# Two attention layers on one core: four score tiles in one run, and long products in 64-column halves

## The chip, the cores and the metric

The kernel runs on one core of one Trainium2 chip. The metric is the device time in microseconds of one execution. Three runs of the kernel before took 3401.60, 3404.48 and 3403.71 us; the median is 3403.71.

## What is computed

32 batches of 512 rows with 512 features go through two layers. All data and products are 32-bit floats.

```python
# layer 0, 8 heads of 64 columns
q, k, v = heads(x @ Wq.T + bq), heads(x @ Wk.T + bk), heads(x @ Wv.T + bv)
logits = q @ k.T / sqrt(64) + log(clip(adj, 1e-8))
out = softmax(logits) @ v                   # (512, 512) per batch
x = layer_norm(x + out @ Wo.T + bo, gamma, beta)
# layer 1, one head
p = x @ fc_w.T + fc_b
qq, kk = p @ q_w.T + q_b, p @ k_w.T + k_b
masked = leaky(qq + kk.T + (1 - adj) * -1e9)
x = softmax(masked) @ p + x
```

## The kernel before

**Slots.** The work of a batch b is divided into four slots, p = 0 to 3, one for each pair of heads (`slot`, L1258). The order of the instructions on each engine is the order in which the program writes them: nothing rearranges it. In one slot the attention of batch b, the end of layer 0 and layer 1 of batch b - 1, and the last products of batch b - 2 are mixed. A slot in the middle of the run takes about 26 us, a batch 105.

**Scores and values.** `score` (L825) multiplies 128 keys with 512 queries for two heads, one on the upper and one on the lower 64 rows of TensorE's array, and ScalarE makes the exponentials of both in one instruction (L836). There are four score tiles in a slot, kc = 0 to 3. `factors` (L839) multiplies them on VectorE by the adjacency, and `sums` (L849) adds them up. `values` (L859) multiplies with v; here the two heads lie on two column tiles of 64 columns each and are accumulated in one bank, `po`. Its second part ends with a copy on ScalarE (L877). The values used in a slot are those of the slot before.

**Divide.** `divide` (L880) sums over keys for four heads, on four column tiles of 32, copies the result (L892) and sends it through DRAM into another shape. `divided` (L900) inverts it and loads it as R, which has one buffer; `scale` (L920) multiplies it in.

**Long products.** Every other product of 512 x 512 matrices is done by a scheme with seven products of half size in place of eight. It needs sums and differences of quarters on VectorE before and after. Each product is written as four matmuls, each with a 128 x 128 left factor and 256 moving columns; the profile shows each as two instructions with two weight loads. They are the queries and keys of the next slot (`seven_qk`, L621, tiles `f`), the values of the next batch (`seven_v`, `pv`), the output projection (`seven_wo`, `pw`), the last product (`seven_out`, `pw_o`), all three through `seven` at L215, and the product with the layer 1 weights (`seven_z`, L998, `pw_z`). `differences` (L594, L602 to L605) makes the quarters of the next batch's x at the beginning of slot 3, for `seven_v` and `seven_qk`.

**Banks.** [...] The pool `ps_s` has two buffers of two banks, for the scores and the tiles `f`; `po` has one; the pool `ps_m` has three, which the other long products and the divide take in turn. A product's three results are called a, b and c. The output projection is seeded with a bias by two copies on ScalarE (`seed`, L749).

**Order of a slot.** TensorE gets: score tiles 0 and 1, the values of the slot before (both parts), score tiles 2 and 3, a divide in slots 0 and 2, then the long products. In slot 2, `layer1_rows` (L1391) orders the rest: sums of batch b for kc 0 and 1 (L1407), the sums for the last product (`z_sums`), dots for layer 1 (`ks`, `qs`), and the last product with its adds. The end of it is this line, and slot 3 begins with the differences:

```python
1439            run(muls[2:3] + adds[2] + muls[3:])
1440            load_e(last, 1)
1441            run(adds[3][:1] + qs + adds[3][1:])
```

DMAs are issued by SyncE, in the order of the program.

Of the kernel before, what the change touches and what calls it, by code (L numbers as in the profile page):

```python
# [9 lines left out]
FP = mybir.dt.float32  # L10
# [9 lines left out]
P = 128  # L20
# [10 lines left out]
def kernel(  # L31
# [173 lines left out]
    def turn_fc():  # L205

        fc12, fc22 = K["fc"][:, :KH, H:], K["fc"][:, KH:, H:]
        nc.vector.tensor_sub(fc12, fc22, fc12)

    def seven(data, weights, i, to, first, ns=range(KH)):  # L210


        for n in ns:
            for c in range(KH):
                nc.tensor.matmul(  # L215
                    to[:, n, :], data(i, c)[:, ts(n, P)], weights[i][:, c, :],
                    start=(first and n == 0 and c == 0),
                    stop=(n == KH - 1 and c == KH - 1), skip_group_check=True,
                )
# [278 lines left out]
    def fast(ctx):  # L498
# [4 lines left out]
        ps_o = ctx.enter_context(tc.tile_pool(name="ps_o", bufs=1, space=bass.MemoryType.PSUM))  # L503
        ps_m = ctx.enter_context(tc.tile_pool(name="ps_m", bufs=3, space=bass.MemoryType.PSUM))
        dram = ctx.enter_context(tc.tile_pool(name="dram", bufs=2, space=bass.MemoryType.DRAM))

        S = [dict() for _ in range(B)]

        def load_x(b):
# [98 lines left out]
        def seven_qk(b, p):  # L608

            qk_tiles(b, p)  # L610
            s = S[b]
            q, k = s["qT", p], s["kT", p]
            bq, bk = K["bq"][:, p : p + 1], K["bk"][:, p : p + 1]
            wq, wk, W = K["wq"], K["wk"], K["qk_s"]
            left = {1: wq[:, :KH], 2: wq[:, KH:], 3: W[:, 2], 4: wk[:, KH:],
                    5: W[:, 0], 6: W[:, 1], 7: wk[:, :KH]}
            ps = {}

            def mul(i, to, first):
                for c in range(KH):  # L620
                    nc.tensor.matmul(  # L621
                        to, left[i][:, c, ts(p, P)], s["B"][i][:, c, :],
                        start=(first and c == 0), stop=(c == KH - 1),
                        skip_group_check=True,
                    )

            def banks():
                f = [ps_s.tile([P, 2, N], FP, tag="s", name=f"f_{b}_{p}_{i}") for i in range(2)]
                for i, name in enumerate("acbd"):
                    ps[name] = f[i % 2][:, i // 2, :H]  # L630

            def unit0():
                banks()
                mul(1, ps["a"], True)
                mul(5, ps["c"], True)
                nc.scalar.copy(ps["b"], ps["a"])
                nc.scalar.activation(k[:, H:], ps["c"], AF.Identity, bias=bk)

            def unit1():
                mul(6, ps["a"], False)
                mul(2, ps["b"], False)
                nc.scalar.activation(q[:, H:], ps["a"], AF.Identity, bias=bq)  # L644
                nc.scalar.activation(q[:, :H], ps["b"], AF.Identity, bias=bq)

            def unit2():
                mul(4, ps["d"], True)
                mul(3, ps["c"], False)
                nc.scalar.activation(k[:, :H], ps["d"], AF.Identity, bias=bk, scale=-1.0)  # L650

            def adds():
                nc.vector.tensor_add(q[:, H:], ps["c"], q[:, H:])
                nc.vector.tensor_add(k[:, H:], ps["a"], k[:, H:])
                nc.vector.tensor_add(k[:, :H], ps["a"], k[:, :H])  # L655
            return [unit0, unit1, unit2, lambda: mul(7, ps["a"], False), adds]

        def seven_v(b):
# [13 lines left out]
            def unit0():  # L672
                for name in "abc":
                    ps[name] = ps_m.tile([P, KH, H], FP, tag="m", name=f"pv_{b}_{name}")
                mul(1, ps["a"], True)
# [59 lines left out]
        def seven_wo(b, banks, apart=False):  # L735
# [12 lines left out]

            def seed():  # L749
                for name, bank in zip("bac", banks()):  # L750
                    ps[name] = bank
                for name, h in (("a", 0), ("c", 1)):
                    bo = K["bo"][:, ts(h, H)].unsqueeze(1).to_broadcast([P, KH, H])
                    nc.scalar.copy(ps[name], bo)

# [11 lines left out]
        def seven_out(b):  # L767
# [30 lines left out]
            muls, adds = seven_rows(data, sub, K["fc_s"], K["fc"], lambda n: ps[n], add, True)  # L798
            muls[0] = lambda unit=muls[0]: unit0(unit)
            adds[2].insert(1, lambda: store(0))  # L800
            adds[3].append(lambda: store(1))
# [10 lines left out]
        def long_banks(b):  # L812
            return lambda: [
                ps_m.tile([P, KH, H], FP, tag="m", name=f"pw_{b}_{name}") for name in "bac"
            ]
# [8 lines left out]

        def score(b, p, kc):  # L825

            s = S[b]
            sc = ps_s.tile([P, 2, N], FP, tag="s", name=f"sc_{b}_{p}_{kc}")
            for j in range(2):
                rows = slice(j * DK, (j + 1) * DK)  # L830
                nc.tensor.matmul(  # L831
                    sc[:, j, :], s["kT", p][rows, ts(kc, P)], s["qT", p][rows, :],
                    start=True, stop=True,
                )
            at = act.tile([P, 2, N], FP, tag="at", name=f"at_{b}_{p}_{kc}", bufs=6)
            nc.scalar.activation(at, sc, AF.Exp, scale=SCALE)  # L836
            s["at", p, kc] = at
# [42 lines left out]
        def divide(b, p):  # L880


            s = S[b]
            ps = ps_m.tile([P, N], FP, tag="m", name=f"ps_{b}_{p}")
            for h in range(4):
# [93 lines left out]
        def seven_z(b):  # L979
# [15 lines left out]
            def mul(i, name, first=False):  # L995
                for m in range(KH):
                    for t in range(KH):
                        nc.tensor.matmul(  # L998
                            ps[name][:, m, :].rearrange("p (c n) -> p c n", c=KH),
                            left[i][:, t, ts(m, P)], right[i][:, :, ts(t, P)],  # L1000
                            start=(first and m == 0 and t == 0),
                            stop=(m == KH - 1 and t == KH - 1), skip_group_check=True,
                        )
# [58 lines left out]
        def find_range():  # L1062
# [19 lines left out]
            def over_partitions():  # L1082
                one = ps_s.tile([P, 2, N], FP, tag="s", name="one")
                nc.tensor.transpose(one[:1, 0, :2], least, ident[:2, :2])
                bad = const.tile([1, 1], FP, name="bad")
                nc.vector.tensor_reduce(bad, one[:1, 0, :2], AX.X, ALU.min)
                flag = const.tile([1, 1], I32, name="flag")
# [22 lines left out]
        def last_layer1(b):  # L1110
# [47 lines left out]
            def rest(range_steps, add_before):  # L1158
                ps = {}

                def mul(i, name, first=False):
                    for m in range(KH):
                        for t in range(KH):
                            nc.tensor.matmul(
                                ps[name][:, m, :], left[i][:, t, ts(m, P)], right[i][:, t, :],
                                start=(first and m == 0 and t == 0),
                                stop=(m == KH - 1 and t == KH - 1), skip_group_check=True,
                            )
# [89 lines left out]
        def slot(b, p):  # L1258
# [8 lines left out]
            if p == 3:  # L1267
                differences(nxt)
            for kc in (0, 1):
                score(b, p, kc)  # L1270
            if p == 1 and last >= 0:
                wos, wo_adds = seven_wo(last, long_banks(last))
                run(wos[:1])
            run(values(b, p - 1) if p > 0 else values(last, 3) if last >= 0 else first_v[1:2])
            if p == 0 and last >= 0:
                scale(last, 0)
                first_difference(last)
            factors(b, p, 0)
            fc_sums = right_units(K["fc"], K["fc_s"]) if b == 1 and p == 1 else []
            if p == 1:  # L1280
                sums(b, p, 0)
                run(fc_sums[:1])
                if last >= 0:
                    scale(last, 2)
                    first_sum(last)
            if p == 2 and last >= 0:
# [6 lines left out]
            for kc in (2, 3):  # L1293
                score(b, p, kc)
            soft = softmax(last) if p == 3 and last >= 0 else []
            run(soft[:1])
            if p == 0 and last >= 0:
                if b >= 2:
                    run(eT(b - 2))
                divide(last, 2)  # L1300
                if b == 1:
# [3 lines left out]
            if p == 3 and last >= 0:  # L1305
                divided(b, 0)
            if p == 2 and b != 1:
                divide(b, 0)
            if p < 3:
# [64 lines left out]
            if p == 3:  # L1374
# [11 lines left out]
                vs[3]()  # L1386
                turn_a((0, 1))
                sums(b, p, 0)
                sums(b, p, 1)

        def layer1_rows(b, next_qk, norm):  # L1391
# [11 lines left out]
            if b == 1:  # L1403
                run(next_qk[2:4])
                divide(b, 0)
            else:
                sums(b, 2, 0)  # L1407
# [31 lines left out]
            run(muls[2:3] + adds[2] + muls[3:])  # L1439
            load_e(last, 1)  # L1440
            run(adds[3][:1] + qs + adds[3][1:])

# [5 lines left out]
        def last_slot(rest):  # L1448
# [11 lines left out]
            for kc in (2, 3):  # L1460
                score(b, 3, kc)
            factors(b, 3, 1)
# [246 lines left out]
```

## Time and profile before

| | |
|---|---|
| median of three runs | 3403.71 us |
| span of the profiled execution | 3402.3 us |
| TensorE matmuls, busy | 3388.8 us, 15358 instructions |
| VectorE, busy | 3013.1 us |
| ScalarE, busy | 1393.7 us |
| score matmuls, L831 | 2048 instructions, 508.8 us |
| value matmuls, L869 | 2048 instructions, 468.1 us |
| divide matmuls, L886 | 504 instructions, 67.1 us |
| a long matmul's weight load of 128 columns, mean | 190 ns |
| a value matmul's weight load of 64 columns, mean | 136 ns |
| an exponential of 128 x 1024, L836, mean | 1022 ns |
| SyncE's queue, DMA share of 16 engines' span | 36.0% |

The busy time of a group is the time in which at least one of its instructions is under way; matmuls overlap, so the mean of one is longer than the step from one to the next. The chain of waits is counted from the end of one instruction to the end of the next. PE stands for TensorE's matmuls, PEld for its weight loads, DVE for VectorE, ACT for ScalarE, SP for SyncE.

### The profile page before, as it was taken

The page shows a single profiled execution, that of the slowest core. Times are in us where ns is not written, and L with a number is a line of the kernel's source. Part 1 is how long each engine was busy: PE and PEld are TensorE (multiplying, and loading weights), DVE is VectorE, ACT ScalarE, POOL GpSimd, SP SyncE. Part 2 cuts the span into 40 slices and gives each one's busy share as a digit, 9 for nine tenths or more (in the row PEclk, how much of TensorE's full clock was granted, in tenths as well). Part 3 has the DMA queues.
Part 4 walks back from the last instruction along what each step waited for, and adds up shares of the span by engine and source line. Part 5 has one row for each costly group of instructions (what it writes and reads, how often), then busy time and mean ns, then how long its engine had stood idle before and what let it go on. Part 6 is the DMA issues. An engine that isn't in the chain of part 4 may idle for free.

```text
span 3402.3 us, 43006 instructions
## 1 busy us (share of the span) xinstructions
PE 3388.8 (100%) x15358; PEld 2350.1 (69%) x15358; DVE 3013.1 (89%) x5284; ACT 1393.7 (41%) x2375; POOL 0.9 (0%) x9
## 2 busy tenths in 40 slices
PE   9999999999999999999999999999999999999999
PEld 5667667776777677766776677667766777677766
DVE  7888989889898898898898988989889898899888
ACT  3443443434433444434444343443444443444433
POOL 0000000000000000000000000000000000000000
PEclk9999999999999999999999999999999999999999
DMA  5234242343333443323424234343343333442321
GB/s 124 54 63 91 60 90 67 57 91 81 70 73 52 88 85 65 81 65 68 91 60 86 67 61 90 66 85 66 57 91 81 69 74 54 85 90 61 81 66 51
DMA packets 881572, 251.48 MB, mean 74 GB/s; under 512 B 806732, under 2 KB 809036, under 8 KB 881352
## 3 DMA queue, kind: packets, MB, share of 16 engines
q1 hardware_dynamic: 881352, 248.67, 36.0%
q8 instruction: 123, 2.02, 0.3%
q14 instruction: 97, 0.79, 0.1%
HBM read 182.46 MB, written 34.65 MB: 64 GB/s over the span
## 4 chain that ended last, share of the span: by engine, by line
PE 97%; DVE 1%; SPq 1%; ACT 0%; DMA 0%; issue 0%; DVEq 0%; ACTq 0%
PE f L621 22%; PE sc L831 14%; PE po L869 13%; PE pw_a L215 7%; PE pw_z_a L998 6%; PE pv_a L215 5%; PE pw_o_a L215 5%; PE pw_c L215 3%; PE pv_b L215 3%; PE pv_c L215 3%; PE pw_o_c L215 3%; PE pw_z_c L998 3%; PE pw_o_b L215 3%; PE ps L886 2%; PE pw_b L215 2%; PE pw_z_b L998 2%
## 5 line engine op out<-in xcount | busy, mean ns | idle before, releaser
L836 ACT ACTIVATE at<-sc 128x1024 f32<-128x1024 f32 x512 | 496.6, 1022 | 601.0 <-PE sc L831 599.8
L844 DVE SCALAR_TENSOR_TENSOR at<-cT,at 128x1024 f32<-128x1024 f32 x512 | 600.3, 1215 | 12.9 <-ACT at L836 12.5
L831 PE MATMUL sc<-qT,kT 64*128 64x512 f32 x2048 | 508.8, 615 | 0.5 <-DVE kT L655 0.4
L869 PE MATMUL po<-at,v 128*64 128x512 f32 x2048 | 468.1, 599 | 0.4 <-DVE at L844 0.3
L831 PEld LDWEIGHTS sc<-qT,kT 64*128 64x128 f32 x2048 | 178.0, 186 | 267.3 <-issue 267.3
L869 PEld LDWEIGHTS po<-at,v 128*64 128x64 f32 x2048 | 135.4, 136 | 317.4 <-issue 313.4
L857 DVE TENSOR_TENSOR as<-as,at 128x1024 f32<-128x1024 f32 x254 | 310.3, 1222 | 5.4
L621 PE MATMUL f<-xT,wq 128*128 128x256 f32 x1016 | 267.4, 386 | 0.5 <-ACT at L836 0.5
L621 PE MATMUL f<-T,qk_s 128*128 128x256 f32 x1016 | 250.3, 379 | 0.0
L621 PEld LDWEIGHTS f<-xT,wq 128*128 128x128 f32 x1016 | 187.7, 190 | 77.1 <-ACT at L836 54.2
L998 PE MATMUL pw_z_a<-eP,n 128*128 128x256 f32 x960 | 226.9, 379 | 1.0 <-DVE n L1035 1.0
L621 PEld LDWEIGHTS f<-T,qk_s 128*128 128x128 f32 x1016 | 192.5, 190 | 27.0 <-ACT at L836 0.4
L998 PEld LDWEIGHTS pw_z_a<-eP,n 128*128 128x128 f32 x960 | 180.2, 190 | 28.2 <-ACT L L1010 1.3
L877 ACT COPY oT<-po 128x512 f32<-128x512 f32 x128 | 75.2, 587 | 288.9 <-PE po L869 288.9
L854 DVE TENSOR_TENSOR as<-at,at 128x1024 f32<-128x1024 f32 x128 | 155.0, 1211 | 1.1
L644 ACT ACTIVATE qT<-f,bq 128x256 f32<-128x256 f32 x127 | 59.6, 469 | 223.5 <-PE f L621 223.5
L650 ACT ACTIVATE kT<-f,bk 128x256 f32<-128x256 f32 x127 | 59.8, 471 | 198.1 <-PE f L621 198.1
L762 DVE TENSOR_TENSOR n<-pw_a,n 128x512 f32<-128x512 f32 x96 | 66.3, 691 | 74.9 <-PE pw_a L215 74.9
L621 PE MATMUL f<-xT,qk_s 128*128 128x256 f32 x508 | 130.4, 379 | 0.0
L621 PE MATMUL f<-T,wk 128*128 128x256 f32 x508 | 130.4, 379 | 0.0
L621 PE MATMUL f<-xT,wk 128*128 128x256 f32 x508 | 130.4, 379 | 0.0
L215 PE MATMUL pv_a<-wv,xT 128*128 128x256 f32 x512 | 124.2, 385 | 0.0
(304 smaller groups left out, 5809.0 us busy)
## 6 DMA issues: line engine op xcount, KB each, us to landing
cT<-in_adj_dram SPq DMA_DIRECT2D x512, 64.0 KB
R<-d SPq DMA_DIRECT2D x126, 256.0 KB
x<-in_x_dram SPq DMA_DIRECT2D x124, 256.0 KB
n<-in_x_dram SPq DMA_DIRECT2D x31, 1024.0 KB
L<-in_adj_dram SPq DMA_DIRECT2D x60, 512.0 KB
eP<-L SPq DMA_DIRECT2D x480, 64.0 KB
out_dram<-yb SPq DMA_DIRECT2D x58, 512.0 KB
w<-dk SPq DMA_DIRECT2D x32, 256.0 KB
```

The lines of the kernel that those rows point to most:

```text
L215: nc.tensor.matmul(to[:, n, :], data(i, c)[:, ts(n, P)], weights[i][:, c, :], start=(first and n == 0 and c == 0), stop=(n == KH - 1 and c ...
L621: nc.tensor.matmul(to, left[i][:, c, ts(p, P)], s["B"][i][:, c, :], start=(first and c == 0), stop=(c == KH - 1), skip_group_check=True,)
L762: nc.vector.tensor_add(to, ps[name], to)
L831: nc.tensor.matmul(sc[:, j, :], s["kT", p][rows, ts(kc, P)], s["qT", p][rows, :], start=True, stop=True,)
L836: nc.scalar.activation(at, sc, AF.Exp, scale=SCALE)
L844: nc.vector.scalar_tensor_tensor(at, cT[:, kc, :].unsqueeze(1).to_broadcast([P, 2, N]), ADJ_MIN, at, ALU.max, ALU.mult,)
L854: nc.vector.tensor_add(s["as", p], s["at", p, 0], s["at", p, 1])
L857: nc.vector.tensor_add(s["as", p], s["as", p], s["at", p, kc])
L869: nc.tensor.matmul(s["po", p][j * DK : (j + 1) * DK, :], s["v"][h // 4][:, kc, ts(h % 4, DK)], s["at", p, kc][:, j, :], start=(kc == 0), s ...
L877: nc.scalar.copy(s["oT"][p], s["po", p])
L886: nc.tensor.matmul(ps[h * BL : (h + 1) * BL, :], ones[:, :BL], s["as", p + h // 2][:, h % 2, :], start=True, stop=True,)
L998: nc.tensor.matmul(ps[name][:, m, :].rearrange("p (c n) -> p c n", c=KH), left[i][:, t, ts(m, P)], right[i][:, :, ts(t, P)], start=(first ...
```

## The change

It has these parts.

1. A function `halves` writes a matmul with a 128-column left factor as two, each with 64 of the columns and with its own half of the output's partitions. All long products of the seven-product scheme use it.
2. The first part of the values goes ahead of score tiles 0 and 1 and the second part behind score tiles 2 and 3; all four score tiles follow each other on TensorE.
3. The third score tile (kc = 2) goes to two single banks, with two exponentials of 512 columns. The first slot and the last one keep the two-bank tile.
4. The pool `ps_m` becomes three fixed tiles, `lone`. The divide always uses `lone[0]`, the third score tile `lone[1]` and `lone[2]`, and the long products take a, c and b in this order; after the last product the list is turned by one.
5. In slot 1, the seed of a goes ahead of the values and that of c behind their second part, and `scale(last, 2)` and `first_sum` go ahead of the factors.
6. The divide goes between score tiles and the values' second part. In slot 0, that puts it ahead of the transposes of `eT` in the program.
7. In slot 3, `turn_a((0, 1))` goes behind the sums. In slot 2, the sums for kc 0 and 1 go from the beginning of `layer1_rows` to between the two halves of the last adds, where b > 1 and the batch is not the last.

```diff
+    def halves(to, left, right, start, stop):
+        for h in range(2):
+            nc.tensor.matmul(
+                to[ts(h, DK)], left[:, ts(h, DK)], right,
+                start=start, stop=stop, skip_group_check=True,
+            )
...
         for n in ns:
             for c in range(KH):
-                nc.tensor.matmul(
+                halves(
                     to[:, n, :], data(i, c)[:, ts(n, P)], weights[i][:, c, :],
-                    start=(first and n == 0 and c == 0),
-                    stop=(n == KH - 1 and c == KH - 1), skip_group_check=True,
+                    first and n == 0 and c == 0, n == KH - 1 and c == KH - 1,
                 )
...
+        ps_l = ctx.enter_context(tc.tile_pool(name="ps_l", bufs=1, space=bass.MemoryType.PSUM))
+        lone = [ps_l.tile([P, N], FP, name=f"m{i}") for i in "xyz"]
+        class Turns:
+            n = 0
+            def tile(self, shape, dtype, **_):
+                self.n += 1
+                return lone[self.n % 3]
+        ps_m = Turns()
...
+            muls[3] = lambda unit=muls[3]: (unit(), lone.insert(0, lone.pop()))
...
         def long_banks(b):
             return lambda: [
-                ps_m.tile([P, KH, H], FP, tag="m", name=f"pw_{b}_{name}") for name in "bac"
+                lone[i].rearrange("p (n f) -> p n f", n=KH) for i in (2, 0, 1)
             ]
...
+        def score(b, p, kc, apart=False):
+            s = S[b]
+            halved = kc == 2 and not apart
+            if halved:
+                parts = lone[1:]
+            else:
+                sc = ps_s.tile([P, 2, N], FP, tag="s", name=f"sc_{b}_{p}_{kc}")
+                parts = [sc[:, j, :] for j in range(2)]
...
-            nc.scalar.activation(at, sc, AF.Exp, scale=SCALE)
+            if halved:
+                for j in range(2):
+                    nc.scalar.activation(at[:, j, :], parts[j], AF.Exp, scale=SCALE)
+            else:
+                nc.scalar.activation(at, sc, AF.Exp, scale=SCALE)
...
+            vals = values(b, p - 1) if p > 0 else values(last, 3) if last >= 0 else []
+            if p == 1 and last >= 0:
+                wos, wo_adds = seven_wo(last, long_banks(last))
+                wos[0]("a")
+            run(vals[:1])
             for kc in (0, 1):
                 score(b, p, kc)
-            if p == 1 and last >= 0:
-                wos, wo_adds = seven_wo(last, long_banks(last))
-                run(wos[:1])
-            run(values(b, p - 1) if p > 0 else values(last, 3) if last >= 0 else first_v[1:2])
...
+            if p == 1 and last >= 0:
+                scale(last, 2)
+                first_sum(last)
             factors(b, p, 0)
             if p == 1:
                 sums(b, p, 0)
                 run(fc_sums[:1])
-                if last >= 0:
-                    scale(last, 2)
-                    first_sum(last)
...
             for kc in (2, 3):
-                score(b, p, kc)
+                score(b, p, kc, first)
+            if p == 0 and last >= 0:
+                divide(last, 2)
+            if p == 2 and b != 1:
+                divide(b, 0)
+            run(vals[1:])
+            if p == 1 and last >= 0:
+                wos[0]("c")
             soft = softmax(last) if p == 3 and last >= 0 else []
             run(soft[:1])
...
                 vs[3]()
-                turn_a((0, 1))
                 sums(b, p, 0)
                 sums(b, p, 1)
+                turn_a((0, 1))
...
             if b == 1:
                 run(next_qk[2:4])
                 divide(b, 0)
-            else:
+            elif nxt == B:
                 sums(b, 2, 0)
...
             load_e(last, 1)
+            if b > 1:
+                sums(b, 2, 0)
             run(adds[3][:1] + qs + adds[3][1:])
```

More of the change, by code (lines that the diff above doesn't have):

```diff
@@ L503, in fast @@
         ps_o = ctx.enter_context(tc.tile_pool(name="ps_o", bufs=1, space=bass.MemoryType.PSUM))
-        ps_m = ctx.enter_context(tc.tile_pool(name="ps_m", bufs=3, space=bass.MemoryType.PSUM))
+        ps_l = ctx.enter_context(tc.tile_pool(name="ps_l", bufs=1, space=bass.MemoryType.PSUM))
         dram = ctx.enter_context(tc.tile_pool(name="dram", bufs=2, space=bass.MemoryType.DRAM))
         S = [dict() for _ in range(B)]
+        lone = [ps_l.tile([P, N], FP, name=f"m{i}") for i in "xyz"]
[5 more added lines that the diff above has]
+        ps_m = Turns()
         def load_x(b):
@@ L620, in mul @@
                 for c in range(KH):
[L621 to L625, printed above, removed]
+                    halves(to, left[i][:, c, ts(p, P)], s["B"][i][:, c, :],
+                           first and c == 0, c == KH - 1)
             def banks():
@@ L672, in unit0 @@
             def unit0():
-                for name in "abc":
-                    ps[name] = ps_m.tile([P, KH, H], FP, tag="m", name=f"pv_{b}_{name}")
+                ps.update(zip("bac", long_banks(b)()))
                 mul(1, ps["a"], True)
@@ L747, in seven_wo, with seed @@
             ps = {}
[L749 to L754, printed above, removed]
+            def seed(names="ac"):
+                if not ps:
+                    ps.update(zip("bac", banks()))
+                for name in names:
+                    bo = K["bo"][:, ts("ac".index(name), H)]
+                    nc.scalar.copy(ps[name], bo.unsqueeze(1).to_broadcast([P, KH, H]))
             def sub(i, a, b):
@@ L823, in other_banks @@
             return tiles
-        def score(b, p, kc):
+        def score(b, p, kc, apart=False):
             s = S[b]
-            sc = ps_s.tile([P, 2, N], FP, tag="s", name=f"sc_{b}_{p}_{kc}")
+            halved = kc == 2 and not apart
[4 more added lines that the diff above has]
+                parts = [sc[:, j, :] for j in range(2)]
             for j in range(2):
@@ L831, in score @@
                 nc.tensor.matmul(
-                    sc[:, j, :], s["kT", p][rows, ts(kc, P)], s["qT", p][rows, :],
+                    parts[j], s["kT", p][rows, ts(kc, P)], s["qT", p][rows, :],
                     start=True, stop=True,
@@ L883, in divide @@
             s = S[b]
-            ps = ps_m.tile([P, N], FP, tag="m", name=f"ps_{b}_{p}")
+            ps = lone[0]
             for h in range(4):
@@ L997, in mul @@
                     for t in range(KH):
-                        nc.tensor.matmul(
+                        halves(
                             ps[name][:, m, :].rearrange("p (c n) -> p c n", c=KH),
                             left[i][:, t, ts(m, P)], right[i][:, :, ts(t, P)],
-                            start=(first and m == 0 and t == 0),
-                            stop=(m == KH - 1 and t == KH - 1), skip_group_check=True,
+                            first and m == 0 and t == 0, m == KH - 1 and t == KH - 1,
                         )
@@ L1082, in over_partitions @@
             def over_partitions():
-                one = ps_s.tile([P, 2, N], FP, tag="s", name="one")
-                nc.tensor.transpose(one[:1, 0, :2], least, ident[:2, :2])
+                po = ps_s.tile([P, 2, N], FP, tag="s", name="pone")
+                nc.tensor.transpose(po[:1, 0, :2], least, ident[:2, :2])
                 bad = const.tile([1, 1], FP, name="bad")
-                nc.vector.tensor_reduce(bad, one[:1, 0, :2], AX.X, ALU.min)
+                nc.vector.tensor_reduce(bad, po[:1, 0, :2], AX.X, ALU.min)
                 flag = const.tile([1, 1], I32, name="flag")
@@ L1163, in mul @@
                         for t in range(KH):
-                            nc.tensor.matmul(
+                            halves(
                                 ps[name][:, m, :], left[i][:, t, ts(m, P)], right[i][:, t, :],
-                                start=(first and m == 0 and t == 0),
-                                stop=(m == KH - 1 and t == KH - 1), skip_group_check=True,
+                                first and m == 0 and t == 0, m == KH - 1 and t == KH - 1,
                             )
@@ L1268, in slot @@
                 differences(nxt)
+            first = b == 0 and p == 0
+            vals = values(b, p - 1) if p > 0 else values(last, 3) if last >= 0 else []
[3 more added lines that the diff above has]
+            run(vals[:1])
             for kc in (0, 1):
                 score(b, p, kc)
-            if p == 1 and last >= 0:
-                wos, wo_adds = seven_wo(last, long_banks(last))
-                run(wos[:1])
-            run(values(b, p - 1) if p > 0 else values(last, 3) if last >= 0 else first_v[1:2])
+            if first:
+                run(first_v[1:2])
             if p == 0 and last >= 0:
@@ L1299, in slot @@
                     run(eT(b - 2))
-                divide(last, 2)
                 if b == 1:
@@ L1306, in slot @@
                 divided(b, 0)
-            if p == 2 and b != 1:
-                divide(b, 0)
             if p < 3:
@@ L1460, in last_slot @@
             for kc in (2, 3):
-                score(b, 3, kc)
+                score(b, 3, kc, True)
             factors(b, 3, 1)
```

## The prediction

> **What bounds the kernel now.** I read the page first, then the chain of waits in order of time for one batch, then the timelines of TensorE, its weight loads and VectorE where the slots meet, and last the list of waits.
>
> ```profile
> PE 3388.8 (100%) x15358; PEld 2350.1 (69%) x15358; DVE 3013.1 (89%) x5284; ACT 1393.7 (41%) x2375; POOL 0.9 (0%) x9
> ...
> PEclk9999999999999999999999999999999999999999
> ```
>
> TensorE is never free and runs at its full granted clock, so the time changes only if TensorE does less, switches less, or is made to wait. VectorE at 89% is the next limit. The chain of waits, one slot (p = 3) of batch 15, says what TensorE's time is made of:
>
> ```profile
> 1525.78 1.92 PE sc L831 x8
> 1527.69 3.58 PE po L869 x16
> 1531.28 1.92 PE sc L831 x8
> 1533.19 1.92 PE pv_a L215 x8
> 1535.12 1.73 PE pv_c L215 x8
> 1536.85 1.73 PE f L621 x8
> ```
>
> The same eight L215 matmuls take 1.73 us after their own kind (0.216 each) and 1.92 after scores: entering costs 0.19. Scores and values run two at a time. Their loads in the timeline show the beat:
>
> ```profile
> 1501.79 0.14 PEld L869 LDWEIGHTS po<-at,v 128*64 128x64 f32 x2 [0.29 <-issue]
> ...
> 1502.22 0.14 PEld L869 LDWEIGHTS po<-at,v 128*64 128x64 f32 x2 [0.28 <-issue]
> ...
> 1502.65 0.14 PEld L869 LDWEIGHTS po<-at,v 128*64 128x64 f32 x2 [0.28 <-issue]
> ```
>
> One pair each 0.43 us. So four score pairs are 1.72 of their 1.92 (entering: 0.20), eight value pairs 3.43 of 3.58 (entering: 0.15). In slots with a divide, its piece of 0.99 is two beats (0.86) plus 0.13, and the products after it (6.24 for 28) are 28 x 0.216 plus 0.19. A slot before the change thus pays 0.20 + 0.15 + 0.20 + 0.19 = 0.74 us for changes of kind, and 0.87 with a divide.
>
> What could stand in TensorE's way is VectorE at the start of slot p = 3:
>
> ```profile
> 1522.71 0.84 DVE L785 SCALAR_TENSOR_TENSOR yb<-pw_o_b,r,yb 128x256 f32<-128x256 f32 x2
> 1523.46 0.87 DVE L785 SCALAR_TENSOR_TENSOR yb<-pw_o_c,r,yb 128x256 f32<-128x256 f32 x2
> 1524.25 1.65 DVE L785 SCALAR_TENSOR_TENSOR yb<-pw_o_a,r,yb 128x256 f32<-128x256 f32 x4
> 1525.81 0.69 DVE L386 SCALAR_TENSOR_TENSOR R<-n,uq 128x512 f32<-128x512 f32 x1
> ...
> 1531.72 0.68 DVE L605 TENSOR_TENSOR xT<-xT 128x512 f32<-128x512 f32 x1
> ```
>
> It works without a gap from 1517 to 1532.4, and the list of waits has
>
> ```profile
> PEld pv_a L215 <- DVE xT L605: 22.0, 29, 0.8
> ```
>
> The first weight load of the next batch's values waits for L605, the last of the four differences. Before, this cost nothing: L605 ends at 1532.40 and the load, held by the scores until then, starts at 1533.12. The reader should see that 0.72 us of room, in 29 batches.
>
> **What the Trainium skill says.** "TensorEngine Tiling (Array Packing)", Key Properties: changing the tiling mode drains the engine, changing only the tile doesn't, and tiles work in parallel. The trace agrees: 0.13 to 0.20 us at each change, none inside a run. "TensorE: Matmul & The Clock Gate", "Wait — 56ns, not 53.3ns?": starts come no closer than about 25 ns however small a matmul is, and about 62 ns per MATMUL where the sequencer decodes in microcode. No run here shows a sustained stream that tight. The same page, "Architectural detail", says that VectorE and ScalarE queues are strictly first in, first out; the timelines agree, each follows the program's order.
>
> **The change part by part.**
>
> *Long products in halves.* The rows of L621, L215, L998 and L1164 hold 10,556 MATMULs with as many loads; each becomes two, side by side on two column tiles. Nearest rows: eight whole-array 128x512 MATMULs at L241 take 3.6 us in all with 592 ns for the last, so (3.6 - 0.59) / 7 = 0.43 each; a value pair of two 64-column tiles at 512 also takes 0.43. Halving costs nothing there, so I take 0.216 per pair at 256. The loads of a pair run together (0.14 for two, against 190 ns for one of 128 columns) and hide behind the 0.216. Unknown is the supply: four instructions per 0.216, 54 ns each, where this trace sustains one per 108; the divide's eight loads within 0.16 us show only that a waiting queue empties fast. Bounds: nothing, up to 4 x 62 = 248 ns per pair by the page's price, 10,556 x 0.032 = +338 us. A gain is excluded, since the same columns stream. I take nothing.
>
> *Order and modes.* A slot is now half the values, four scores, [divide], half the values, long products, and all but scores and divide have one mode. It pays 0.20 (scores) + 0.15 (values) = 0.35, or with a divide 0.20 + 0.13 + 0.15 = 0.48. Saved: 0.39 in either. Of 128 slots the first has no values and the last keeps the old order: 126 x 0.39 = 49 us.
>
> *Four scores in a run.* Two big buffers serve scores 0, 1 and 3; score 2 goes to two lone banks with two exponentials. The first exponential ends about 1.1 + 1.02 = 2.1 us after the first score's matmuls begin, the fourth score's matmuls start at 3 x 0.86 = 2.57: no wait. The split costs ScalarE one more instruction, from the 587 ns of a 128x512 copy against 1022 at most 0.15 us per slot; it is hidden by ScalarE's 41% and by the 1.72 us of second half values. Without that cover it would hold the next slot's first bank, 0.15 x 126 = 19 us. The lone banks are free in time: the last reader in slot 0's end is L1048 (1578.33 + 0.68), the third score writes over 3.6 us after that slot's start at about 1578.2.
>
> *Seed in two parts (p = 1).* The second seed (0.60) follows the copy of po (about 0.5 until the next may start), behind the last values; its product comes 1.73 after them. 0.2 + 0.5 + 0.6 = 1.3: hidden by the first product, with little over 0.1 left once its load is issued a beat ahead.
>
> *scale and first_sum (p = 1) ahead of the factors.* They now stand where VectorE would be at 1580.15. Their input R is issued at 1577.98 and 1578.69, and its packets run to about 1581.8, so VectorE waits some 1.8 us, and the factors and sums queue behind it. The factors end near 11.5 us into the slot (10.0 before). TensorE wants first_sum at 7.2 (done near 5.9) and the following subtraction near 13.9: hidden. Slack gone would cost 1.8 x 31 = 56 us.
>
> *divide earlier, turn_a after the sums.* The divide needs the sums of slot 3; without the two transposes (1.21) ahead they end 5.1 us into slot 0, the divide stands at 5.4. Its copy then waits for the scale at 7.6 because R has one buffer, and so sits ahead of po's copy and f's; both are needed only later. SP's store is issued about 1 us earlier, still behind the spread of eP. Cost nothing; otherwise 1 us in 31 slots.
>
> *sums(b, 2, 0) moved to the end of slot 2.* One L854 of 1.22 us goes from 1510.5, where it was before z_sums, to between the two halves of the four adds at 1524.25. It comes too late to be absorbed: the place it leaves only lets VectorE wait for TensorE. The chain ends the products read at 1520.70 and 1524.25 at 1520.60 and 1524.05, so VectorE gets ahead by only 0.07. Behind it in the queue are the adds, the four dots, the last add and the differences; L605 ends at 1532.40 + 1.22 - 0.07 = 1533.55. TensorE, now without switch at the slot's start (1525.61), is ready for the v products 1.72 + 0.20 + 3.43 + 0.15 + 1.72 = 7.22 later, at 1532.83. From the release to the load 0.06 (as in batch 1's slot, 166.55 to 166.61), and 0.05 for the uncovered load (a value run's first beat is 0.48, the others 0.43): start at 1533.66. TensorE waits 0.83 us, 29 times: +24 us. Bounds: nothing, if something pulls VectorE ahead, to 1.0 us (29 us). I take 0.83. The spread and everything behind this in slot 3 comes about 0.7 later against TensorE and is caught by the gaps that VectorE has before 1547.3 and 1551.56 (0.97).
>
> **Sum.** -49 + 24 = -25 us. The span 3402.3 becomes 3377; the median 3403.71 is 1.4 above the span, so 3379.
>
> **Rivals.**
> *Full gain:* the stall at L605 doesn't come, since VectorE finds its 1.2 us. For it: VectorE idles 11% of the time; against: none of it lies in this stretch. 3403.7 - 49 = 3355. Chance 0.20.
> *Slower, a pair takes longer than one whole product:* place, every long product; if the second tile's start (7 ns behind in po's pairs) isn't hidden, 10,556 x 0.007 = +74, so 3379 + 74 = 3453; with 62 ns per instruction 3717. It outweighs the gain from 25 / 10,556 = 2.4 ns per pair. Against it: L241 and po agree at 0.43. Chance 0.14.
> *The modes aren't one:* long products and values still drain between them. Then a slot pays 0.15 + 0.20 + 0.15 + 0.19 = 0.69, saving 0.05 x 126 = 6, and L605 still costs 0.83 - 0.34 = 0.49 x 29 = 14: 3412. That is the change not doing what it says. Chance 0.06.
> *Small new waits* (second seed, z's third product, which has 1.0 us of waits now at L1035, eP's landing): 0.2 in each of 126 slots eat the 25: 3404. Chance 0.07.
> The forecast has 0.53.
>
> **How the numbers follow.** Below 0.2% (7 us) nothing can be told from no change. Faster: 0.53 + 0.20 less a little, 0.72. Same: the small waits and edges, 0.10. Slower: 0.14 + most of 0.06, 0.18. The forecast's own range is 3372 to 3386; to hold 8 in 10 it must reach full gain (3355, with 5 for its terms) and the modes' rival: 3350 to 3412, leaving out the slow pair.
>
> **What would show it.** Right: long MATMULs in pairs, 0.216 apart; no step of 0.19 between po and them; scores at 3.63 for 16; a TensorE gap of about 0.8 us at the v products behind L605 in 29 slots. Wrong: pairs above 0.22, drains left between po and products, L605 early, or waits on ACT at L836 within the scores.

## The result and the profile after

Twelve runs of the changed kernel have a median of 3400.39 us (3397.40 to 3405.44), and twelve of the kernel before 3403.09 us. The ratio is 0.9994 with a 95% interval of 0.9985 to 1.0002: no difference that can be told. The profiled executions have spans of 3402.3 before and 3398.7 after. The forecast was 3379, within 3350 to 3412.

The page of the changed kernel, first the busy times, then the shares of the chain of work that ended last, and these shares in the kernel before:

```profile
PE 3349.1 (99%) x25914; PEld 1914.6 (56%) x25914; DVE 3007.2 (88%) x5284; ACT 1394.7 (41%) x2501; POOL 0.9 (0%) x9
...
PE 81%; DVE 9%; SPq 5%; DMA 3%; issue 1%; ACT 1%; DVEq 0%; ACTq 0%
```

```profile
PE 97%; DVE 1%; SPq 1%; ACT 0%; DMA 0%; issue 0%; DVEq 0%; ACTq 0%
```

TensorE's busy time fell by 39.7 us and the span by 3.6. So work or switching did leave TensorE, and idle time came in. The shares say where from: 9% of the chain is now VectorE, 5% is SyncE's queue (SPq) and 3% is DMA, where VectorE and that queue had 1% each.

Now the chain at the stretch that the prediction showed, slot 3 of batch 15 in time order (mx, my and mz are the three tiles of `lone`):

```profile
1523.40 1.72 PE po L891 x8
1525.11 1.92 PE sc L849 x8
...
1527.89 0.86 PE sc L849 x4
1528.75 1.87 PE po L891 x8
1530.61 1.73 PE mz L213 x16
1532.34 1.73 PE mx L213 x16
1534.07 1.73 PE f L213 x16
```

The first values enter with no extra (1.72 for eight). The four scores run as one: two take 1.92, the fourth 0.86, and the third, in the lone banks, the 0.86 between them (1527.03 to 1527.89, left out above). The second values pay 0.15 (1.87). The first product of v follows with no extra, at 1.73 for sixteen instructions, where eight took 1.92. This is the slot as forecast, with one exception: nothing waits in front of `mz`, the first product of v. VectorE was at that time here:

```profile
1530.48 0.69 DVE L621 TENSOR_TENSOR xT<-xT 128x512 f32<-128x512 f32 x1
```

L621 is the fourth difference, which was L605 before. It ends at 1531.16, and the first product of v is then over half a microsecond old.

To see what all slots paid, I took from the trace the steps between the starts of successive matmul groups and subtracted the beat of their size (0.216 or 0.429 us). What is left over is sorted by size: 60 to 140 ns is counted as a change of kind, more as a wait. These limits are a choice, and a change of kind can also leave part of its cost in steps below 60 ns. The beats alone come to 3276.6 us in each kernel listed.

| us over the whole run | changes of kind | below 60 ns | waits |
|---|---|---|---|
| before | 100.0 | 7.3 | 7.8 |
| after | 51.7 | 9.6 | 50.9 |

48.3 us of changes went, and 43.1 us of waits came. 33.6 of the waits stand in one place, before the third product with layer 1's weights, in 30 slots p = 0. The chain there, batch 16:

```profile
1665.57 1.79 DVE eP L572 x3
1667.36 0.02 issue
1667.39 0.69 DVE R L1048
1668.08 0.60 DVE third L1049
1668.68 1.15 DVE yb L464
1669.83 0.02 issue
1669.85 0.69 DVE n L1052
1670.54 0.60 DVE eP L1055
1671.14 0.61 DVE n L1056
1671.76 0.14 issue
1671.89 1.95 PE my L213 x16
```

`eP` holds the weights of layer 1's softmax, rearranged by DMAs and then transposed. VectorE has no gap from its transposes (L572) to the subtraction L1056 that the product needs. Hence the lateness lies ahead of L572. VectorE's timeline and two lines of the list of waits say what it stood waiting for; the last line is from the kernel before, where the transposes are L556:

```profile
1661.04 2.35 DVE L866 SCALAR_TENSOR_TENSOR at<-cT,at 128x1024 f32<-128x1024 f32 x2
1664.86 2.49 DVE L572 STREAM_TRANSPOSE eP<-eP 128x512 f32<-128x512 f32 x4 [1.47 <-DMA d<-R]
```

```profile
DVE oT L946 <- DMA R<-d: 96.7, 31, 4.7
...
DVE eP L572 <- DMA d<-R: 48.3, 30, 3.6
```

```profile
DVE eP L556 <- DMA d<-R: 1.9, 1, 1.9
```

L572 waited 1.47 us here, 48.3 in all, in 30 batches; before, the transposes waited once, 1.9 us. The name `d<-R` must not be taken literally: L572 reads `eP`. SyncE's queue in that slot:

```profile
1643.26 0.35 SPq L934 DMA_DIRECT2D d<-c  x1
1644.70 1.31 SPq L937 DMA_DIRECT2D R<-d  x2
1646.06 4.79 SPq L542 DMA_DIRECT2D cT<-in_adj_dram  x8
1650.94 11.91 SPq L148 DMA_DIRECT2D eP<-L  x16
1662.96 0.56 SPq L917 DMA_DIRECT2D d<-R  x1
```

`eP` is written by sixteen DMAs, the spread, whose issues alone take 11.91 us; the last ends at 1662.85, and L572 starts 2.01 us after that. SyncE does one thing after another: the divisor's store (`d<-c`), R's two loads, eight loads of `cT` (adjacency for kc 2 and 3), the spread, and the store `d<-R`, which merely comes next. The same chain over the 30 batches that have a spread, medians in us; a minus is time before slot 0's first matmul:

| | before | after |
|---|---|---|
| store of the divisor, after slot 3's start | 14.45 | 15.70 |
| length of slot 3 | 25.75 | 25.35 |
| first issue of the spread | -3.54 | -1.32 |
| last issue ends | 7.90 | 9.92 |
| transposes of `eP` start | 10.30 | 11.96 |
| from the last issue's end to that start | 2.39 | 2.00 |

The spread ends 2.02 us later against TensorE: 1.25 because VectorE reaches the divisor later, 0.40 because slot 3 got shorter, the remaining 0.37 in SyncE's queue. If 2.00 us are what the data take to be there, VectorE came to the transposes 0.39 us after them before. That room is gone, and 1.6 us of wait stand in its place, 30 times.

### The profile page after: what moved, and what is told of

Same layout as the page of the kernel before. It is cut to its first block, busy times and chain, and to the rows that moved or that the text cites. A ratio compares the mean times of both kernels' runs of the same rounds, so it can differ in the third digit from the quotient of the medians.

```text
span 3398.7 us, 64226 instructions
## 1 busy us (share of the span) xinstructions
PE 3349.1 (99%) x25914; PEld 1914.6 (56%) x25914; DVE 3007.2 (88%) x5284; ACT 1394.7 (41%) x2501; POOL 0.9 (0%) x9
## 4 chain that ended last, share of the span: by engine, by line
PE 81%; DVE 9%; SPq 5%; DMA 3%; issue 1%; ACT 1%; DVEq 0%; ACTq 0%
PE f L213 17%; PE mx L213 13%; PE my L213 13%; PE mz L213 13%; PE po L891 12%; PE sc L849 9%; SPq L148 3%; DVE eP L572 2%; DMA d<-R 1%; DVE at L866 1%; PE my L849 1%; SPq L542 1%; DVE yb L464 1%; PE mz L849 1%; DMA d<-c 1%
## 5 line engine op out<-in xcount | busy, mean ns | idle before, releaser
L849 PE MATMUL sc<-qT,kT 64*128 64x512 f32 x1544 | 387.5, 607 | 0.0
L213 PE MATMUL f<-xT,wq 128*64 128x256 f32 x2032 | 262.4, 379 | 0.0
L213 PE MATMUL f<-T,qk_s 128*64 128x256 f32 x2032 | 251.6, 379 | 0.6 <-ACT f L651 0.6
L213 PEld LDWEIGHTS f<-xT,wq 128*64 128x64 f32 x2032 | 146.0, 137 | 100.6 <-issue 28.0
L213 PEld LDWEIGHTS f<-T,qk_s 128*64 128x64 f32 x2032 | 145.7, 137 | 74.6 <-ACT f L651 1.4
L946 DVE TENSOR_TENSOR oT<-oT,R 128x512 f32<-128x512 f32 x126 | 80.2, 677 | 96.7 <-DMA R<-d 96.7
L213 PE MATMUL f<-T,wk 128*64 128x256 f32 x1016 | 131.2, 379 | 0.0
L213 PE MATMUL f<-xT,wk 128*64 128x256 f32 x1016 | 131.2, 379 | 0.0
L213 PE MATMUL f<-xT,qk_s 128*64 128x256 f32 x1016 | 131.2, 379 | 0.0
L213 PE MATMUL mz<-eP,n 128*64 128x256 f32 x960 | 115.6, 380 | 10.8 <-DVE n L1056 8.1
L213 PE MATMUL mx<-eP,n 128*64 128x256 f32 x960 | 115.6, 380 | 10.4 <-DVE n L1056 9.2
L572 DVE STREAM_TRANSPOSE eP<-eP 128x512 f32<-128x512 f32 x120 | 74.7, 681 | 48.3 <-DMA d<-R 48.3
```

Of the source, the lines that this page charges most:

```text
L213: nc.tensor.matmul(to[ts(h, DK)], left[:, ts(h, DK)], right, start=start, stop=stop, skip_group_check=True,)
L572: lambda c=c: nc.vector.transpose(dst[:, c, :], src[:, c, :]) for c in range(4)
L849: nc.tensor.matmul(parts[j], s["kT", p][rows, ts(kc, P)], s["qT", p][rows, :], start=True, stop=True,)
L946: nc.vector.tensor_mul(oT, oT, s["R", p][:, k, :])
```

## The experiments

Each was run in three rounds beside the kernel before, whose medians in these comparisons were 3402.8 to 3403.7 us.

| | median us | ratio, 95% interval | changes of kind | waits |
|---|---|---|---|---|
| after | 3400.39 | 0.9994 [0.9985, 1.0002] | 51.7 | 50.9 |
| sums back | 3372.36 | 0.9911 [0.9895, 0.9928] | 51.4 | 20.9 |
| spread first | 3356.48 | 0.9863 [0.9847, 0.9879] | 50.9 | 10.5 |
| divide later | 3397.73 | 0.9985 [0.9977, 0.9994] | 52.0 | 46.3 |
| order only | 3409.65 | 1.0018 [1.0011, 1.0026] | 89.1 | 19.9 |
| halves only | 3400.30 | 0.9991 [0.9982, 1.0000] | 89.0 | 10 |
| before, spread first | 3401.51 | 0.9995 [0.9989, 1.0002] | 99.9 | 6.3 |
| both | 3364.04 | 0.9883 [0.9867, 0.9900] | 50.6 | 16.8 |
| spread first, no split | 3428.20 | 1.0073 [1.0057, 1.0090] | 65.7 | 60.5 |
| spread first, scale behind | 3370.38 | 0.9903 [0.9887, 0.9920] | 51.9 | 22.7 |

**The sums for kc 0 and 1 back at the start of `layer1_rows`** (changed kernel, one part undone).

```diff
-            elif nxt == B:
+            else:
                 sums(b, 2, 0)
...
-            if b > 1:
-                sums(b, 2, 0)
```

> The changed kernel, with the sums for kc 0 and 1 of slot 2 back at the beginning of layer1_rows. Theory A (VectorE is 1.15 us later in slot 3, so SyncE issues the spread of eP later, the transposes of eP in slot 0 wait for it, 48 us in the trace, and the z product's third matmuls wait for VectorE, some 42 us): the spread starts about 1.1 us earlier against slot 0, the wait before the transposes falls below 20 us, the z waits below 15 us, time 3370 to 3380. Theory B (the transposes wait for the divide's transfer, which now stands ahead of them in the program): nothing changes, 3400.

It is 28 us faster than the changed kernel. The store of the divisor is back at 14.67 after slot 3's start and the spread ends at 8.69; the transposes start 2.01 later, and their wait has shrunk:

```profile
DVE eP L572 <- DMA d<-R: 10.5, 18, 2.9
```

So the place of the sums does cost time, by way of the spread and not of the differences. But the chain shows a wait of its own, in slot 2, before a later one of the last product's seven:

```profile
1503.22 1.73 PE mx L213 x16
1504.94 0.02 issue
1504.96 1.95 PE my L213 x16
```

**The loads of `cT` behind the spread** (changed kernel; the only edit is in SyncE's order).

```diff
             if p == 3:
-                load_a(nxt, (2, 3))
                 vs = seven_v(nxt)
...
                 run(soft[2:])
+                load_a(nxt, (2, 3))
```

> The changed kernel, with the loading of the second half of the next adjacency (kc 2, 3) behind the spread of eP on SyncE in slot 3. Theory A: the spread starts as soon as the weights are there, some 2.5 us earlier, the transposes no longer wait, the z waits vanish but for a few us, and the 49 us of saved mode changes appear: 3355 to 3365. Theory B: the same as the changed kernel, 3400.

It takes 43.9 us off the changed kernel: 46.5 us below the kernel before, which is nearly the whole saving in changes of kind (49.1 in this kernel). First its page's chain shares, then SyncE in batch 15, and the same stretch in the changed kernel and in the kernel before:

```profile
PE 96%; DVE 2%; DMA 1%; ACT 1%; issue 0%; SPq 0%; DVEq 0%; ACTq 0%
```

```profile
1520.02 0.35 SPq L934 DMA_DIRECT2D d<-c  x1
1521.47 2.20 SPq L937 DMA_DIRECT2D R<-d  x2
1525.87 10.78 SPq L148 DMA_DIRECT2D eP<-L  x16
1536.69 5.33 SPq L542 DMA_DIRECT2D cT<-in_adj_dram  x8
```

```profile
1542.68 4.54 SPq L542 DMA_DIRECT2D cT<-in_adj_dram  x8
1547.32 10.79 SPq L148 DMA_DIRECT2D eP<-L  x16
```

```profile
1542.96 4.66 SPq L526 DMA_DIRECT2D cT<-in_adj_dram  x8
1547.71 11.48 SPq L148 DMA_DIRECT2D eP<-L  x16
```

Slot 0 begins at 1529.85, 1548.74 and 1551.52 in the three. So the spread begins 3.98, 1.42 and 3.81 us ahead of it. The divisor is as late as in the changed kernel (15.69 after slot 3's start, median): VectorE is not a bit earlier, only SyncE has less in front of the spread. The trace shows what the spread then waits for. In batch 15 ScalarE finishes the last of the weights (L447) at 1525.75, and the spread starts 0.12 us later; in the changed kernel they are finished at 1544.63 and the spread starts 2.69 us later, after the loads of `cT`. VectorE then goes from factors to transposes without a wait, and in the chain the products with layer 1's weights follow each other at 1.73 us:

```profile
1537.82 2.35 DVE L866 SCALAR_TENSOR_TENSOR at<-cT,at 128x1024 f32<-128x1024 f32 x2
1540.09 2.48 DVE L572 STREAM_TRANSPOSE eP<-eP 128x512 f32<-128x512 f32 x4
```

The median from the last issue to L572 is 3.04 us here: about 1 us of room. TensorE's waits fall from 50.9 to 10.5 us.

**The divide of slot 0 behind the transposes again** (changed kernel). The rival theory was that the earlier divide, whose store `d<-R` the list names, makes L572 wait.

```diff
             if p == 0 and last >= 0:
+                if b >= 2:
+                    run(eT(b - 2))
                 divide(last, 2)
...
-                if b >= 2:
-                    run(eT(b - 2))
```

> The changed kernel with slot 0's divide behind the transposes of eP in the program, as before. Theory A (the transposes wait for the spread of eP, which is late): no change, 3397 to 3404. Theory B (they wait for the divide's transfer, issued ahead of them): the wait goes, 3355 to 3370.

```profile
DVE eP L572 <- DMA d<-R: 42.2, 29, 4.2
```

The wait stays, with the store now behind L572 in the program, and the transposes still start 2.01 us after the last issue of the spread. That theory falls, and so does the name in the list.

**The order without the halves** (changed kernel, whole 128-column matmuls).

```diff
-        for h in range(2):
-            nc.tensor.matmul(
-                to[ts(h, DK)], left[:, ts(h, DK)], right,
-                start=start, stop=stop, skip_group_check=True,
-            )
+        nc.tensor.matmul(to, left, right, start=start, stop=stop, skip_group_check=True)
```

> The changed kernel with the long products as whole 128-column matmuls again: the order alone. If the modes explain the saving, a slot pays 0.15 + 0.20 + 0.15 + 0.20 = 0.70 us against 0.74 before, 5 us saved in all, and the late spread still makes z wait, but less as a slot is 0.34 us longer: 3405 to 3430. If halving itself has a hidden price, this run is faster than the changed kernel, under 3395.

**The halves without the order** (kernel before, all four places of long products through `halves`).

```diff
-                    nc.tensor.matmul(
-                        to, left[i][:, c, ts(p, P)], s["B"][i][:, c, :],
-                        start=(first and c == 0), stop=(c == KH - 1),
-                        skip_group_check=True,
-                    )
+                    halves(to, left[i][:, c, ts(p, P)], s["B"][i][:, c, :],
+                           first and c == 0, c == KH - 1)
```

> The kernel before with the long products in halves and nothing else. If halves cost nothing: one shorter entry (0.10 in place of 0.19) behind the scores or the divide, 0.05 x 126 = 6 us saved: 3395 to 3400. If a pair takes longer than a whole product by even 3 ns: 3425 or more.

Either alone takes 11 us out of the steps of 60 to 140 ns, but 6 to 7 us come back in steps below 60 ns (13.7 us of them with the order only, 14.1 with the halves only, 7.3 before). So either alone saves 4 to 5 us, about what was expected of it; together they remove 48. With whole products there is a change between values and products as well, and with the old order there are scores in front of both. Halves alone lose nothing (3400.3): a pair takes no longer than one whole product. The order alone ends 6.7 us above the kernel before (0.11% to 0.26% of it), since its 12 us of new waits exceed what it saves. Of its waits, 11.2 us stand before the third product with layer 1's weights, and VectorE waits 21.0 us for `eP` in 20 batches.

**The same move of the loads in the kernel before**, as a control.

> The kernel before, with only the loading of kc 2 and 3 of the next adjacency behind the spread of eP. Before, the transposes hardly wait for eP and TensorE not at all, so nothing is to be had: 3399 to 3405. If the spread's place is worth 44 us by itself, under 3370.

There is no gain that can be told (0.9995, interval 0.9989 to 1.0002): TensorE didn't wait for the spread before. The 44 us aren't a gain that lay ready in the old kernel; they are what the change lost to that queue.

**Both: sums back and spread first.**

> The changed kernel with both: the sums of slot 2 back at the beginning of layer1_rows, and the spread ahead of the adjacency. If one late spread was the whole loss, the two don't add: 3353 to 3362. If the sums in their old place cost TensorE something of their own (6 us of waits stand before the last product's L213 matmuls in the run with the sums back), it is slower than the spread alone by up to 6 us.

It is 7.6 us slower than the spread alone, more than the 6 expected at most. The list of waits has loads of the last product that wait for L791, which now queues behind the sums (one bank; the other two have 7.1 and 6.6):

```profile
PEld my L213 <- DVE L L791: 7.2, 19, 0.6
```

So the new place of the sums is right, worth 7.6 us once SyncE's order fits; with SyncE's order as it was, it costs 28.

**The third score not split** (on the version with the spread first).

```diff
-            halved = kc == 2 and not apart
+            halved = False
```

> The changed kernel with the spread first, and with the third score tile in the two-bank pool like the others, one exponential each. The third tile's matmuls then wait for the first exponential, from 1.9 to 2.4 us after the run's beginning: 0.5 us in 125 slots, 60 us: 3410 to 3425. If the split isn't needed: 3356.

It costs 72 us, 0.57 in each of 126 slots, where 60 were expected. The timeline of TensorE shows the run of scores breaking on ScalarE, with two big buffers for four tiles:

```profile
1509.72 1.99 PE L849 MATMUL sc<-qT,kT 64*128 64x512 f32 x8
1511.98 2.04 PE L849 MATMUL sc<-qT,kT 64*128 64x512 f32 x8 [0.27 <-ACT at L858]
```

54.5 of its 60.5 us of waits lie between two scores. The rest of the 72 is mostly steps of 60 to 140 ns, 14.8 us more than with the split. The two lone banks are what lets four scores run together.

**`scale` and `first_sum` behind the factors and sums of slot 1 again** (on the same version).

```diff
-            if p == 1 and last >= 0:
-                scale(last, 2)
-                first_sum(last)
             factors(b, p, 0)
             if p == 1:
                 sums(b, p, 0)
                 run(fc_sums[:1])
+                if last >= 0:
+                    scale(last, 2)
+                    first_sum(last)
```

> The changed kernel with the spread first, and in slot 1 scale(last, 2) and first_sum back behind the factors and the sums. VectorE's 91 us of waits for R then go. If they were hidden as forecast: the same as with the spread first alone, 3354 to 3359. If the wait mattered: faster by up to 30 us. If the output projection needs first_sum earlier than VectorE then reaches it (it ended at 7.7 us into the slot before, and TensorE now gets there at 7.2, the second product at 8.9): waits at L770's readers, up to 0.5 us in 30 slots, 3360 to 3372.

It costs 13.9 us. TensorE waits 13.3 us, in 31 slots, before the output projection's second product, and the list names `first_sum` (L961), with 3.2 us for one bank and 2.4 for each of the others.

So having VectorE wait for R is cheaper than having TensorE wait for VectorE.

## Why the prediction was wrong

**Right: the changes of kind.** The saving was put at 126 x 0.39 = 49 us, and 48.3 was measured. The property that the prediction took from the Trainium skill ("TensorEngine Tiling (Array Packing)", Key Properties: a change of the tiling mode drains, a change of tile doesn't) holds here: the step between values and half products is gone, the one between values and whole products isn't (order only: 0.10 us, 127 times).

**Right: halves cost nothing.** The group of the queries' and keys' products in the page, then the pace:

```profile
L213 PE MATMUL f<-T,qk_s 128*64 128x256 f32 x2032 | 251.6, 379 | 0.6 <-ACT f L651 0.6
```

The pairs of the last product (`mx<-fc,L`) start at 1511.139, 1511.355, 1511.571 and 1511.787 in one stretch of the trace, 0.216 apart, the pair's second 7 ns behind each. The bound of +338 us from the price per MATMUL (the Trainium skill, "TensorE: Matmul & The Clock Gate", "Wait — 56ns, not 53.3ns?") isn't met. The page prices a MATMUL; that the two weight loads cost as much (4 x 62) was the prediction's own step, and by the page's price the two MATMULs alone come to an estimated 124 ns, less than the 216 measured. The rival of a 7 ns penalty per pair falls too.

**Right: the split, the seed and the divide.** No score's matmuls wait for a bank: between two scores no step is more than 140 ns over the beat. The trace has 2.0 us of waits in all (4 slots) between the output projection's first and second product, where the seed could have come late. The divide's copy of R waits until 7.5 us into slot 0 (1556.20 of a slot begun at 1548.74; forecast 7.6) and holds nobody.

**Right in kind, too small: VectorE's wait for R.** It was put at 1.8 x 31 = 56 us and measured 96.7, 3.1 each, hidden all the same. What was too small is the time until R is there: from the end of its two issues to VectorE's start 3.80 us pass (median of the 31), where the prediction counted 2.5 (1579.29 to 1581.8, the end of the packets). The experiment shows the other side, 13.9 us for the old order.

**Wrong: "TensorE waits 0.83 us, 29 times: +24 us"** (step *sums(b, 2, 0) moved to the end of slot 2*). The delay of VectorE was right: the last difference ended 6.62 us after slot 3's start before (1532.40 less 1525.78) and 7.76 after (1531.16 less 1523.40), 1.14 more for 1.15 forecast. But v's first product doesn't read L605's result. In the code, product 1 takes the quarter b11, which no difference writes, and product 7 alone takes what the fourth difference leaves; the chain shows the matmuls of product 1 before that difference ends. "PEld pv_a L215 <- DVE xT L605" named the last VectorE event ahead of the load, and I built 24 us on it without asking which operand the load reads.

**Wrong, and this decided: "The spread and everything behind this in slot 3 comes about 0.7 later against TensorE and is caught by the gaps that VectorE has"** (same step). It looked for the catch on VectorE alone. What follows the divisor is SyncE's queue, where 26 issues (R's two, `cT`'s eight, the spread's sixteen) take 17.75 us in batch 15, from 1540.36 to 1558.11, with no gap to catch anything. The spread came 2.0 later, not 0.7, and the room at its consumer was 0.39 (2.39 less 2.00). The 2.39 stood in SyncE's and VectorE's timelines before, and I did not take it. This term was put at nothing; it is some 40 of the 43 us of new waits on TensorE, those that go when the spread comes first. Moving one group of issues, with VectorE's order left alone, gives 43.9 back.

The result lies where the rival "small new waits" put it (3404; it named eP's landing and z's third product), at a chance of 0.07. That rival named a right place, but priced it as 0.2 us in each of 126 slots, where some 1.1 us stand in each of 30, and gave no mechanism. That 3400 lies in the stated range is luck: the range's upper end stood for the modes not being one. Full gain (3355) is what the kernel reaches with the spread first, 3356.48: the change was worth that much, and the rest of the forecast's sum was one wait that didn't come and one that wasn't seen.

Not settled: what the further 0.37 us in SyncE's queue are made of. A spread takes 11.39 us to issue (median) in the changed kernel and 10.79 before, because more of the spreads hold an issue that takes over 0.8 us in place of 0.63, up to 2.0 (17 of 30, before 11 of 30); why single issues take so long stays open. In batch 15 R's two issues took 0.96 longer (2.27 for 1.31), but their median is 1.31 in both kernels.

## What to carry to other kernels

When TensorE gets shorter by some tenths of a us per stage, or VectorE's work moves towards a DMA's source, follow the queue of DMA issues up to the data's first reader and write down the room there (landing to reader); here it was spent first. Order the issues on such a queue by when their data is due: here 64 KB loads with time to spare stood ahead of the transfer on which everything hung. And before a wait in a list is priced, read in the code which operand the waiting instruction takes; the name in the list is only the event that came last.

## What was not expected of the hardware

TensorE sustained four instructions (two loads, two matmuls) per 0.216 us, 54 ns each, for whole products on end; the kernel before shows one per 108 ns in its long products.

The issue itself is what takes SyncE's time in these stretches: 0.67 us for each of the spread's DMAs (10.79 / 16) and 0.57 for each of `cT`'s (4.54 / 8), with 64 KB in both. From the last issue's end to the first reader 2.00 or 2.01 us pass (medians) in the four kernels in which that reader mostly waits: after, sums back, divide later, order only. "DMA: Bandwidth & Descriptors" in the Trainium skill ("Anatomy of one DMA — SWDGE (gpsimd) path") gives some 2.0 us as a transfer's fixed part for another issuing engine; what is measured here, from SyncE, is the time behind the issue, and it is as constant.
